# One core, banded attention and a 4-bit feed-forward: dequantization's steps placed behind the first row tiles, b2 copied ahead, transposes fixed behind products, mask loads later

## The chip, the cores and the metric

The kernel runs on one core of one Trainium2 chip. The metric is device time in microseconds (us) of one execution, the median of three runs; the profile is of one further execution, and says when each instruction of each engine began and ended. TensorE (PE) multiplies and transposes, VectorE (DVE) and ScalarE (ACT) work on elements, GpSimd (POOL) does the same for small pieces, SyncE (SP) issues most of the DMAs. Each engine takes its instructions strictly in the order in which they were put into its queue, and waits for semaphores of the others.

## The reference

Four batches of 512 rows of 1024 numbers (2048 rows in all) go through two layers, each followed by a residual sum and a layer norm:

```python
attn = jnp.einsum('ds,td->st', w1, w2) * sparse_mask        # 1024 x 1024, zero outside a band
y    = jax.nn.gelu(jnp.einsum('bds,st->bdt', x, attn) + b2, approximate=False)
x    = _layernorm(x + y)

e    = jnp.linalg.norm(x, axis=-1)
mask = e > 64.0                                             # rows that would take 8-bit weights
y    = where(mask, x @ dequant(qweight, lut8, 8).T, x @ dequant(qweight, lut4, 4).T) + bias
x    = _layernorm(x + y)
```

`dequant` reads bit p of each weight's code from plane p (32 weights to a word) and looks the code up in a table of its own for every output row: 16 entries with 4 bits.

## The kernel before

Rows are handled in 16 tiles of 128 (`x_tiles[0..15]`), columns in 8 blocks of 128 (`KT = 8`) or two halves of 512. The kernel computes the 4-bit product for all rows, and a band of `attn` only; alongside, it checks that no row's norm is over 64 and that the mask is zero outside the band (`outside_band`, `check_outside`, `count_odd`). Were one of the two to fail, `general_path` would compute everything anew. It doesn't with these inputs.

**Stage 1, attn (lines 400 to 486).** Eight column windows s = 0..7, each at most 268 wide: 8 matmuls over k into a PSUM tile (L454), a multiplication by the mask on DVE (L476) into `attn[:, s]`. The matmuls need `w2` transposed: eight tiles of it are loaded by SP into three buffers, transposed on PE into PSUM (L281), and copied to `w2T` by ACT (L282). `w1` comes in pieces of one, one, two, two and two windows into two buffers. The transposes of tile s + 2 stand in the middle of window s, behind its fourth matmul. Beside that the first two row tiles are transposed (`first_xT`).

**Dequantization (lines 281 to 345).** A generator, `dequantize_all`, yields 16 times: twice for each of the 8 blocks of output columns (`ot`). For a pair of blocks DVE first shifts the code words into bytes (`v`, L297, 8 instructions); then for each block and side, ACT computes three entries (`e`, L322) and POOL one (`root`, L326), each as one linear function of bit 0, and DVE selects among them by bits 1 to 3 (L329, L330, L331, L335) and adds the identity to the block of the diagonal (L338), so that the residual comes out of the product. One step later the finished block is transposed on PE and copied by ACT into `wT` (`transpose_pending`). `steps(1)` advances the generator by one yield, and the place of the call in the program decides how soon the scheduler takes its instructions. Before, `steps(1)` stands at the end of each of the 8 windows of stage 1, and 8 more behind the entries of `unpack_after` in stage 2.

**Stage 2, a list of entries `todo`.** Attention of tile n (`attention`): ACT copies b2, spread over all partitions, into a PSUM tile (L526), 10 matmuls add the banded product (L532), ACT applies Gelu (L557), DVE adds the row tile and sums (L561), ACT squares and sums (L380), POOL takes the inverse root (L382, L383), DVE normalizes (L387). "left" and "right" entries are the feed-forward halves of tiles 0 to 3: 8 matmuls of 512 columns (L575), each against one half of `wT`; "left" 0 needs blocks 0 to 3 of `wT`. Each entry's transposed input is prepared one entry ahead (`prepare`). The PSUM tiles of stages 1 and 2 share two buffers (`ps_mm`), the transposes four (`ps_tr`). Row tiles 2 to 11 are loaded into memory that stage 1's tiles leave, so their first load waits for the last of stage 1's instructions.

**Stage 3, pairs of row tiles.** Tiles 4 to 15 go in six pairs through a seven-product form of the 2 x 2 block product (`ffn_pair`, L692). Their inputs are rearranged by `squares`: a DVE transpose in 32 x 32 squares (L642), one DMA out to DRAM (L646) and four back (`rows`, L652), then copies and sums (L674 to L679). `load_outside` loads the parts of the mask outside the band into the places of tiles 0 to 3 (L516), ACT sums their absolute values (L521).

The order within each engine's queue is made by a scheduler from the program's order and its own estimates; from `("attention", 8)` on DVE's is the program's. `tc.issue_after(i)` puts every instruction of its block that goes to the engine of `i` behind `i` in that engine's queue.

Of the kernel before, what the change touches and what calls it, by code (L numbers as in the profile page):

```python
# [9 lines left out]
FP = mybir.dt.float32  # L10
# [7 lines left out]
P = 128  # L18
D = 1024
SOON = 12  # L20
PAIR = 2
KT = D // P
# [11 lines left out]
AHEAD = 2  # L34
# [158 lines left out]
def kernel(  # L193
# [13 lines left out]
    nc = tc.nc  # L207
# [7 lines left out]
    with ExitStack() as main:  # L215
# [48 lines left out]
        b2_bc = const.tile([P, D], FP, name="b2_bc")  # L264
# [20 lines left out]
        def transpose_columns(dst, src):  # L285
            return transpose_blocks(dst, lambda k: src[:, ts(k, P)])
# [81 lines left out]
        def steps(n):  # L368
            for _ in range(n):
                next(low, None)  # L370
# [31 lines left out]
        with tc.tile_pool(name="prod", bufs=1) as prod:  # L402
            w2T = prod.tile([P, KT, D], FP, name="w2T")
            w1_cols = w1.rearrange("(k p) s -> p k s", p=P)
            w2_raw, w1_sb, masks = {}, {}, {}
            first_xT = []

            def load_w2(t):
                w2_raw[t] = prod.tile([P, D], FP, tag="w2", name="w2_raw", bufs=3)
                nc.sync.dma_start(out=w2_raw[t], in_=w2[ts(t, P), :])  # L410

            def load_w1(first, n):

                t = prod.tile([P, KT, n * P], FP, tag=f"w1_{n}", name="w1_sb", bufs=2)
                nc.sync.dma_start(out=t, in_=w1_cols[:, :, first * P : (first + n) * P])
                for s in range(first, first + n):
                    w1_sb[s] = t[:, :, ts(s - first, P)]
                    lo, hi = window(s)
                    masks[s] = prod.tile([P, WIN], FP, tag="mask", name="mask", bufs=6)
                    nc.sync.dma_start(out=masks[s][:, : hi - lo], in_=sparse_mask[ts(s, P), lo:hi])  # L420

            load_w2(0)
            load_w2(1)
            load_w1(0, 1)

            nc.scalar.activation(warm, warm, AF.Gelu)
            load_w2(2)
            load_w1(1, 1)
            load_entries(2, KT, nc.sync)
            load_w2(3)  # L430
            load_w1(2, 2)
            load_codes(0)
            load_codes(1)
            load_w2(4)
            load_codes(2)
            load_codes(3)
            load_w2(5)
            load_w1(4, 2)
            load_w2(6)
            load_w2(7)  # L440
            load_w1(6, 2)
            for n in range(AHEAD):
                load_x(xp0, n)
            nc.sync.dma_start(out=b2_bc, in_=b2.partition_broadcast(P))

            transpose_columns(w2T[:, :, ts(0, P)], w2_raw[0])
            done = transpose_columns(w2T[:, :, ts(1, P)], w2_raw[1])
            behind = ExitStack()
            behind.enter_context(tc.issue_after(done.ins))
            for s in range(KT):  # L450
                lo, hi = window(s)
                ps = ps_mm.tile([P, D], FP, tag="mm", name="mm")
                for k in range(KT):
                    part = nc.tensor.matmul(  # L454
                        out=ps[:, : hi - lo],
                        lhsT=w1_sb[s][:, k, :],
                        rhs=w2T[:, k, lo:hi],
                        start=(k == 0),
                        stop=(k == KT - 1),
                    )  # L460
                    if k == KT // 2 - 1 and s + 2 < KT:
                        with tc.issue_after(part.ins):
                            transpose_columns(w2T[:, :, ts(s + 2, P)], w2_raw[s + 2])
                if s >= KT - 2:


                    for a, b, begins in ((hi - lo, HALF, False), (HALF, D, True)):
                        nc.tensor.matmul(
                            out=ps[:, a:b],
                            lhsT=zeros[:, :P],  # L470
                            rhs=zeros[:, a:b],
                            start=begins,
                            stop=True,
                            skip_group_check=True,
                        )
                nc.vector.tensor_tensor(  # L476
                    attn[:, s, : hi - lo], ps[:, : hi - lo], masks[s][:, : hi - lo], ALU.mult
                )
                if s >= KT - 2 - AHEAD and len(first_xT) < AHEAD:

                    n = len(first_xT)
                    xT = work.tile([P, D], FP, tag="z", name="xT", bufs=2)
                    first_xT.append(xT.rearrange("p (k r) -> p k r", k=KT))
                    transpose_columns(first_xT[n], x_tiles[n])
                steps(1)
            behind.close()

        late = main.enter_context(tc.tile_pool(name="late", bufs=1))
        for n in range(AHEAD, SOON):
# [24 lines left out]
        def load_outside(s):  # L514
            for raw, row, a, b, _ in outside_band(s):
                nc.sync.dma_start(out=raw, in_=sparse_mask[row : row + P, a:b])  # L516

        def check_outside(s):

            for raw, _, _, _, i in outside_band(s):  # L520
                nc.scalar.activation(raw, raw, AF.Abs, accum_out=outside[:, i : i + 1])  # L521

        def band_rows(xT):

            ps = ps_mm.tile([P, D], FP, tag="mm", name="mm")
            nc.scalar.copy(ps, b2_bc)  # L526
            for s in range(KT):
                lo, hi = window(s)
                for h in range(NH):
                    a, b = max(lo, h * HALF), min(hi, (h + 1) * HALF)  # L530
                    if a < b:
                        nc.tensor.matmul(  # L532
                            out=ps[:, a:b],
                            lhsT=xT[:, s, :],
                            rhs=attn[:, s, a - lo : b - lo],
                            start=False,
                            stop=hi == D or (h == 0 and window(s + 1)[0] >= HALF),
                            skip_group_check=True,
                        )
            return ps  # L540
# [31 lines left out]

        def product(ps, xT, h):
            for k in range(KT):
                nc.tensor.matmul(  # L575
                    out=ps,
                    lhsT=xT[:, k, :],
                    rhs=wT[:, k, ts(h, HALF)],
                    start=(k == 0),
                    stop=(k == KT - 1),  # L580
                )
# [49 lines left out]
        def weight_sum(pool, i):  # L631
# [3 lines left out]
            minus = weights[minus] if isinstance(minus, int) else minus  # L635
            nc.vector.tensor_tensor(weights[i], plus, minus, ALU.subtract)

        def squares(pool, n):


            t = pool.tile([P, Q, KT, SQ], FP, tag="squares", name="squares")
            nc.vector.transpose(  # L642
                out=t, in_=x_tiles[n].rearrange("t (c j k) -> t c k j", c=Q, k=KT)
            )
            there = moved.tile([Q, SQ, Q, KT * SQ], FP, tag="there", name="there", bufs=4)
            nc.sync.dma_start(  # L646
                out=there.rearrange("a j c e -> (a j) (c e)"),
                in_=t.rearrange("p c k r -> p (c k r)"),
            )
            rows = pool.tile([P, Q, KT, SQ], FP, tag="rows", name="rows", bufs=2)  # L650
            for c in range(Q):
                nc.sync.dma_start(  # L652
                    out=rows[ts(c, SQ), :, :, :].rearrange("j a k r -> j a (k r)"),
                    in_=there[:, :, c, :].rearrange("a j e -> j a e"),
                )
            return rows.rearrange("p a k r -> p k a r")
# [153 lines left out]
        todo += [("attention", n) for n in range(4 + EARLY, SOON)]  # L810
        for m in range(EARLY):
            todo += [("right", m), ("attention", SOON + m)]
        unpack_after = [("attention", 1), ("left", 0), ("attention", 4), ("left", 1)]
        unpack_after += [("attention", 5), ("left", 2), ("attention", 6), ("left", 3)]

        kept = {}
        rows, blocks = {}, {}
# [14 lines left out]

        def prepare(what, n):
            if what == "attention":
                return first_xT[n] if n < AHEAD else transposed(n, "xT", 2, False)
            if what == "left":
                kept[n] = transposed(n, f"early{n}", 1, True)
            return kept[n]

        ready = prepare(*todo[0])  # L840
# [34 lines left out]
        for n in range(EARLY, NT, PAIR):  # L875
            m = n - EARLY - PAIR
            if 0 <= m < KT:
                for s in range(m, m + PAIR):
                    load_outside(s)
            if n == NT - PAIR:  # L880
                count_all(count_odd())
            ffn_pair(ps_pair, n, blocks[n], lambda part, m=n + PAIR: prepare_pair(m, part))
# [44 lines left out]
```

## Time and profile before

| | |
|---|---|
| three runs | 358.59, 359.25, 360.48 us; median 359.25 |
| the profiled execution, its own time | 360.45 us |
| its span on the core | 358.7 us |
| mean granted clock of TensorE | 0.973 |
| ACT, idle time ahead of its lookups (L322) | 12.6 us, 11.0 of it until DVE's `v` (L297) |
| ACT: 58 to 86 us, 86 to 148 us | busy 19.44 of 28, 53.93 of 62 |
| PE: 58 to 86 us, 86 to 148 us, 148 to 201 us, 201 to 351 us | busy 22.93 of 28, 60.58 of 62, 53.00 of 53, 146.21 of 150 |

In the slices of the page, each digit is the busy share of one fortieth of the span (9 us). A group names its line, engine, operation, result and operands; "idle before" says how long the engine stood idle just ahead of such instructions and what ended it. The granted clock tells at what share of its full rate TensorE was allowed to run.

### The profile page before, as it was taken

The page shows a single profiled execution, that of the slowest core. Times are in us where ns is not written, and L with a number is a line of the kernel's source. Part 1 is how long each engine was busy: PE and PEld are TensorE (multiplying, and loading weights), DVE is VectorE, ACT ScalarE, POOL GpSimd, SP SyncE. Part 2 cuts the span into 40 slices and gives each one's busy share as a digit, 9 for nine tenths or more (in the row PEclk, how much of TensorE's full clock was granted, in tenths as well). Part 3 has the DMA queues.
Part 4 walks back from the last instruction along what each step waited for, and adds up shares of the span by engine and source line. Part 5 has one row for each costly group of instructions (what it writes and reads, how often), then busy time and mean ns, then how long its engine had stood idle before and what let it go on. Part 6 is the DMA issues. An engine that isn't in the chain of part 4 may idle for free.

```text
span 358.7 us, 3719 instructions
## 1 busy us (share of the span) xinstructions
PE 329.9 (92%) x1228; PEld 205.7 (57%) x1228; DVE 214.5 (60%) x341; ACT 179.4 (50%) x257; POOL 90.9 (25%) x131
## 2 busy tenths in 40 slices
PE   7799867598999999999999998999999999999990
PEld 7688756495765759966656643443444443444450
DVE  0589898546997885436476853653644535634342
ACT  3795893978958988974346311303214114024020
POOL 1630431425013442312312530401304004004010
PEclk9899998879999999999999999999999999999996
DMA  8999207700000000320264425153554450441103
GB/s 250 320 320 384 80 0 288 298 2 0 0 0 2 1 0 3 126 111 26 79 215 165 140 80 175 58 199 100 199 177 137 188 175 8 189 154 58 58 3 125
DMA packets 28475, 43.90 MB, mean 122 GB/s; under 512 B 7584, under 2 KB 20640, under 8 KB 28448
## 3 DMA queue, kind: packets, MB, share of 16 engines
q1 hardware_dynamic: 26832, 42.66, 34.9%
q10 hardware_dynamic: 1616, 0.93, 0.9%
q8 instruction: 11, 0.18, 0.2%
q14 instruction: 16, 0.13, 0.1%
HBM read 28.90 MB, written 14.68 MB: 122 GB/s over the span
## 4 chain that ended last, share of the span: by engine, by line
PE 60%; ACT 12%; DMA 11%; DVE 8%; issue 3%; POOL 2%; SPq 2%; ACTq 0%; POOLq 0%; DVEq 0%
PE u L692 15%; PE mm L532 12%; PE mm L575 12%; PE w L692 8%; ACT e L322 6%; PE pt L281 5%; PE v L692 4%; PE mm L454 4%; DMA rows<-there 3%; ACT junk L380 2%; DMA q<-in_L_ffn_qweight_dram 2%; DMA x<-in_L_attn_x_dram 2%; DMA there<-squares 1%; DMA w_sb<-in_L_attn_w_dram 1%; SPq L652 1%
## 5 line engine op out<-in xcount | busy, mean ns | idle before, releaser
L532 PE MATMUL mm<-attn,xT 128*128 128x198 f32 (+2 forms) x320 | 62.5, 353 | 6.9 <-ACT mm L526 6.9
L380 ACT ACTIVATE junk<-x,nm 128x1024 bf16<-128x1024 f32 x31 | 35.7, 1151 | 59.7 <-DVE nm L377 57.3
L532 PEld LDWEIGHTS mm<-attn,xT 128*128 128x128 f32 x320 | 54.8, 197 | 14.6 <-ACT mm L526 7.6
L322 ACT ACTIVATE e<-v,lt,diff 128x1024 f32<-128x1024 uint8 x48 | 56.8, 1243 | 12.6 <-DVE v L297 11.0
L575 PE MATMUL mm<-wT,xT 128*128 128x512 f32 x128 | 56.4, 593 | 1.0 <-ACT wT L282 1.0
L326 POOL TENSOR_SCALAR root<-v,diff,lt 128x1024 f32<-128x1024 uint8 x16 | 31.3, 1965 | 57.9 <-DVE v L297 26.2
L692 PE MATMUL u<-t,halves 128*128 128x512 f32 x96 | 43.3, 593 | 1.0 <-DVE x L712 1.0
L575 PEld LDWEIGHTS mm<-wT,xT 128*128 128x128 f32 x128 | 23.7, 190 | 28.1 <-issue 26.1
L382 POOL TENSOR_SCALAR r<-ss 128x1 f32<-128x1 f32 x31 | 10.4, 334 | 108.8 <-ACT junk L380 108.6
L674 ACT COPY halves<-rows 128x1024 f32<-128x1024 f32 x6 | 6.3, 1048 | 55.4 <-DMA rows<-there 55.4
L454 PE MATMUL mm<-w2T,w_sb 128*128 128x268 f32 (+1 forms) x128 | 30.8, 391 | 2.2 <-ACT w2T L282 2.2
L692 PEld LDWEIGHTS u<-t,halves 128*128 128x128 f32 x96 | 18.2, 190 | 24.3 <-issue 22.5
L678 POOL TENSOR_TENSOR halves<-halves 128x512 f32<-128x512 f32 x6 | 9.5, 1585 | 84.5 <-DVE halves L675 68.3
L642 DVE STREAM_TRANSPOSE squares<-x 128x1024 f32<-128x1024 f32 x12 | 24.3, 2029 | 11.0 <-DMA there<-squares 11.0
L387 DVE TENSOR_SCALAR x<-x,nm,r 128x1024 f32<-128x1024 f32 x16 | 13.0, 813 | 29.0 <-POOL r L383 29.0
L330 DVE COPY_PREDICATED root<-v,e 128x1024 f32<-128x1024 uint8 x16 | 23.3, 1457 | 8.0 <-POOL root L326 4.6
L454 PEld LDWEIGHTS mm<-w2T,w_sb 128*128 128x128 f32 x128 | 23.8, 197 | 6.2 <-ACT w2T L282 2.7
L281 PE MATMUL pt<-ident,x 128*128 128x128 f32 x160 | 21.8, 281 | 4.0 <-DVE x L387 4.0
L561 DVE SCALAR_TENSOR_TENSOR x<-z,x 128x1024 f32<-128x1024 f32 x16 | 21.4, 1335 | 6.2 <-ACT z L557 6.2
L329 DVE COPY_PREDICATED e<-v,e 128x1024 f32<-128x1024 uint8 x16 | 21.3, 1329 | 3.5 <-ACT e L322 3.5
L281 PEld LDWEIGHTS pt<-ident,x 128*128 128x128 f32 x160 | 19.4, 152 | 5.9 <-DVE x L387 4.3
L282 ACT COPY xT<-pt 128x512 f32<-128x512 f32 x40 | 21.4, 591 | 2.3 <-PE pt L281 2.3
(93 smaller groups left out, 438.5 us busy)
## 6 DMA issues: line engine op xcount, KB each, us to landing
x<-in_L_attn_x_dram SPq DMA_DIRECT2D x16, 512.0 KB, 7.4
out_dram<-o SPq DMA_DIRECT2D x14, 512.0 KB, 2.6
there<-squares SPq DMA_DIRECT2D x12, 512.0 KB, 3.1
rows<-there SPq DMA_DIRECT2D x48, 128.0 KB, 2.9
w_raw<-in_L_attn_w_dram SPq DMA_DIRECT2D x8, 512.0 KB, 6.8
w_sb<-in_L_attn_w_dram SPq DMA_DIRECT2D x3, 1024.0 KB, 6.9
w_sb<-in_L_attn_w_dram SPq DMA_DIRECT2D x2, 512.0 KB, 7.2
x<-_L_attn_sparse_mask_dram SPq DMA_DIRECT2D x2, 413.0 KB, 3.7
```

What stands on the lines that cost most here:

```text
L281: nc.tensor.transpose(pt[:, j, :], block(g * (HALF // P) + j), ident)
L282: done = nc.scalar.copy(dst[:, g * (HALF // P) : (g + 1) * (HALF // P), :], pt)
L322: nc.scalar.activation(entry[j], plane(0), AF.Identity, scale=d_k, bias=l_k)
L326: nc.gpsimd.tensor_scalar(entry[j], plane(0), d_k, l_k, ALU.mult, ALU.add)
L330: nc.vector.copy_predicated(root, plane(1), entry[1])
L380: nc.scalar.activation(junk, u, AF.Square, bias=nm, accum_out=ss)
L454: part = nc.tensor.matmul(out=ps[:, : hi - lo], lhsT=w1_sb[s][:, k, :], rhs=w2T[:, k, lo:hi], start=(k == 0), stop=(k == KT - 1),)
L532: nc.tensor.matmul(out=ps[:, a:b], lhsT=xT[:, s, :], rhs=attn[:, s, a - lo : b - lo], start=False, stop=hi == D or (h == 0 and window(s + ...
L561: nc.vector.scalar_tensor_tensor(xt, z, 1.0, xt, ALU.mult, ALU.add, accum_out=total)
L575: nc.tensor.matmul(out=ps, lhsT=xT[:, k, :], rhs=wT[:, k, ts(h, HALF)], start=(k == 0), stop=(k == KT - 1),)
L642: nc.vector.transpose(out=t, in_=x_tiles[n].rearrange("t (c j k) -> t c k j", c=Q, k=KT))
L692: nc.tensor.matmul(out=ps, lhsT=a[:, k, :], rhs=b[:, k, :], start=start and k == 0, stop=stop and k == KH - 1, skip_group_check=True,)
```

## The change

Five edits. (a) The block that keeps ACT's work of dequantization behind the transposes of stage 1 now begins behind the third transposed tile of `w2`, not the second. (b) The last two windows of stage 1 have no `steps(1)`; the steps stand behind attention of tiles 0 to 6 and "left" 0 to 2 instead, ten in all with six in stage 1. (c) The b2 copies of the first two attention entries are written right behind stage 1 (`fill_b2`), ahead of the dequantization steps that follow; further entries copy b2 as before. (d) The transposes that prepare an entry stand behind the last matmul that was traced (`behind_mm`). (e) The mask's loads stand behind the latest `rows` load in SP's queue (`behind_rows`).

```diff
             transpose_columns(w2T[:, :, ts(0, P)], w2_raw[0])
-            done = transpose_columns(w2T[:, :, ts(1, P)], w2_raw[1])
+            transpose_columns(w2T[:, :, ts(1, P)], w2_raw[1])
             behind = ExitStack()
-            behind.enter_context(tc.issue_after(done.ins))
             for s in range(KT):
...
                     if k == KT // 2 - 1 and s + 2 < KT:
                         with tc.issue_after(part.ins):
-                            transpose_columns(w2T[:, :, ts(s + 2, P)], w2_raw[s + 2])
+                            done = transpose_columns(w2T[:, :, ts(s + 2, P)], w2_raw[s + 2])
+                        if s == 0:
+                            behind.enter_context(tc.issue_after(done.ins))
...
-                steps(1)
+                if s < KT - 2:
+                    steps(1)
             behind.close()
+        with_b2 = []
+
+        def fill_b2():
+            ps = ps_mm.tile([P, D], FP, tag="mm", name="mm")
+            nc.scalar.copy(ps, b2_bc)
+            with_b2.append(ps)
+
+        for _ in range(2):
+            fill_b2()
...
+        behind_mm = [part]
+
         def band_rows(xT):
-            ps = ps_mm.tile([P, D], FP, tag="mm", name="mm")
-            nc.scalar.copy(ps, b2_bc)
+            if not with_b2:
+                fill_b2()
+            ps = with_b2.pop(0)
...
-                        nc.tensor.matmul(
+                        behind_mm[0] = nc.tensor.matmul(
                             out=ps[:, a:b],
...
         def product(ps, xT, h):
             for k in range(KT):
-                nc.tensor.matmul(
+                behind_mm[0] = nc.tensor.matmul(
...
+        behind_rows = [None]
         def squares(pool, n):
...
             for c in range(Q):
-                nc.sync.dma_start(
+                behind_rows[0] = nc.sync.dma_start(
...
-        unpack_after = [("attention", 1), ("left", 0), ("attention", 4), ("left", 1)]
-        unpack_after += [("attention", 5), ("left", 2), ("attention", 6), ("left", 3)]
+        unpack_after = [("attention", n) for n in range(7)] + [("left", n) for n in range(3)]
...
             if what == "attention":
-                return first_xT[n] if n < AHEAD else transposed(n, "xT", 2, False)
+                if n < AHEAD:
+                    return first_xT[n]
+
+                with tc.issue_after(behind_mm[0].ins):
+                    return transposed(n, "xT", 2, False)
             if what == "left":
-                kept[n] = transposed(n, f"early{n}", 1, True)
+                with tc.issue_after(behind_mm[0].ins):
+                    kept[n] = transposed(n, f"early{n}", 1, True)
             return kept[n]
...
             if 0 <= m < KT:
-                for s in range(m, m + PAIR):
-                    load_outside(s)
+                with tc.issue_after(behind_rows[0].ins):
+                    for s in range(m, m + PAIR):
+                        load_outside(s)
```

In the queues as they come out, stage 1's first lookups stand behind six copies of `w2T` on ACT, where four stood; the first b2 copy stands right behind the copies of `wT` block 0, the second two lookups later, where 6 lookups and the copies of block 1 stood between. On DVE the mask multiplication of the last window stands three selects and one addition earlier. On PE the transposes of block 1 stand behind the second attention entry, and those of block 4 inside "left" 0. From attention of tile 7 on, PE's order is the same in both. On SP the mask's loads, which stood among the first `out` and `rows` DMAs, stand behind the `rows` of tiles 7, 9, 11 and 13.

## The prediction

> **What bounds the kernel now.** I read the page first. PE is busy 92% of the span, and the slices show that it leaves little after the first fifth; so a change can win what PE stands idle, what it runs at half clock, or nothing.
>
> ```profile
> span 358.7 us, 3719 instructions
> PE 329.9 (92%) x1228; PEld 205.7 (57%) x1228; DVE 214.5 (60%) x341; ACT 179.4 (50%) x257; POOL 90.9 (25%) x131
> ...
> PE   7799867598999999999999998999999999999990
> ...
> PEclk9899998879999999999999999999999999999996
> ```
>
> Next, whom PE waits for. The columns are the waiter, the one waited for, the total, how often, and the longest.
>
> ```profile
> PE mm L532 <- ACT mm L526: 6.9, 3, 5.5
> PE pt L281 <- DVE x L387: 4.0, 1, 4.0
> PE mm L454 <- ACT w2T L282: 2.2, 2, 2.0
> PE u L692 <- DVE x L712: 1.0, 1, 1.0
> PE u L692 <- ACT a L677: 0.9, 1, 0.9
> ```
>
> Two waits hold half of PE's idle time between its first instruction and 350 us (18.2 us, summed over the timeline's brackets): 5.49 us for a b2 copy before attention's first band, 4.04 us for a normalized row tile. The timelines place them and show why the copy is late: ACT works off six lookups and two copies (47.41 to 55.16) that stand ahead of it.
>
> ```profile
> 49.71 1.04 PE L281 MATMUL pt<-ident,root 128*128 128x128 f32 x8
> 56.24 5.33 PE L532 MATMUL mm<-attn,xT 128*128 128x198 f32 x20 [5.49 <-ACT mm L526]
> ```
>
> ```profile
> 47.41 6.92 ACT L322 ACTIVATE e<-v,lt,diff 128x1024 f32<-128x1024 uint8 x6
> 54.21 1.06 ACT L282 COPY wT<-pt 128x512 f32<-128x512 f32 x2
> 55.16 1.98 ACT L526 COPY mm<-b_bc 128x1024 f32<-128x1024 f32 x2
> ```
>
> Idle time costs twice. Below are windows of 3.4 us: length, PE's busy time and instructions, granted clock, DMA share, GB/s. Where PE was busy 1.38 or less of 3.40 us, the next window ran at 0.50; after 1.65 it kept 1.00.
>
> ```profile
> 11.50:14.90 3.40, 1.38 (x9) 0.99 1.15 314
> 14.90:18.30 3.40, 3.40 (x8) 0.50 1.23 330
> 49.10:52.50 3.40, 1.65 (x13) 1.00 0.00 0
> 52.50:55.90 3.40, 0.00 (x0) 0.99 0.11 11
> 55.90:59.30 3.40, 3.06 (x8) 0.51 0.88 337
> ```
>
> **The change, part by part.** I follow the changed queues from stage to stage with durations of this trace. Back to back, the timelines give per instruction: lookup 1.15 us (three in 3.51), copy out of PSUM 0.47, b2 copy and Gelu 0.92, squaring 1.15 to 1.25, select on DVE 1.21, residual 1.22, normalization 0.75; on PE eight transposes 0.87, a band 3.60, a half product 6.87.
>
> *Edit (a).* The copies of the third w2 tile end near 11.9 instead of 15.1, so the 2.02 us wait at 14.72 goes and those matmuls run 12.70 to 14.50. But the next transposes need w2 tile 3, issued at 10.50 and landed 6.7 us later: PE stands from 14.5 to 17.2, where before the transposes began at 18.3. That is 1.1 us ahead if the clock stays, 0.6 behind if it falls (3.4 us at half rate cost 1.7). Either way little reaches the end: DVE's next `v` was done at 37.66, and with the same selects behind the same loads I get 37.7 (38.8 if the clock fell). I take 0, bounds 0 and a 1.1 us loss. The Trainium skill ("TensorE: Matmul & The Clock Gate", Part 1) lets the clock fall only after at least one idle window of some 3.4 us; by it a stop of 2.7 us costs nothing. The trace disagrees: the 2.02 us stop at 12.70 was enough, so I keep the loss as a bound.
>
> *Edits (b) and (c), the first copy.* From 37.75, ACT now runs three lookups (41.2), three copies (42.6), three lookups (46.05), two `wT` copies (47.0) and the b2 copy (47.95). PE, whose last transposes wait for a copy until 41.65, ends stage 1 at 42.1 + 2.7 (three quarters of a window of 3.60) + 2.7 (the last window) + two zero fills of 0.33 = 48.2. The first band starts there, at full clock, and ends at 51.8; before, 56.24 to 61.41. Ahead by 9.6 us.
>
> *What follows the wait.* The row tiles' loads wait for DVE's last mask product (54.39, loads from 54.85). Three selects and an addition fewer put it at about 50.3; the load, 3.3 us from issue to landing, is there at 53.9, and its transposes, which now stand inside the second band, wait 0.6 us. The second band, the transposes of block 1 and of tile 3 end at 58.8, against 66.8. Then comes the new wait. The third b2 copy stands behind, on ACT: Gelu 0 (53.25), lookup, two copies, lookup (56.55), squaring 0 (57.8), Gelu 1 (58.7), lookup (59.85), three copies (61.3), squaring 1, which needs DVE's mean of tile 1 (61.95, behind a normalization, a residual and a select), copy (63.6). It ends at 64.5. So PE stands 5.7 us and restarts at half clock; third band 64.5 against 74.43 before, with 0.87 us of transposes not yet done that were done before.
>
> *Where that goes.* Here ACT and DVE set the pace, not PE: block 3 is finished on DVE at 65.5 (60.9 before), because its steps now interleave with attention. ACT reaches the `wT` copies of blocks 2 and 3 at 79.5; "left" 0 starts there, not at 85.49, after 3.8 us of PE idle. Six of its eight matmuls run, then the transposes of block 4 wait for DVE (about 86.1), and at half clock PE arrives at 86.3 anyway. The fifth band starts at 90.65; before, 93.35. The rest is PE's own work with one wait of 0.7 us for a b2 copy; before it had 0.66 and 0.76 (119.48 and 133.59). Block 5 now is done earlier as well, so both orders have done the same by attention of tile 8: 133.5 against 138.16. **4.66 us ahead**, or 5.96 with no fall of the clock at 79.5.
>
> *Contention.* POOL's lookup takes 1.19 us alone and 2.27 (9.07 for four) where DVE is busy; one took 4.73, and a select took 2.23. Between 60 and 86 us they stand close together (two of block 5 around an inverse root). From nothing to 2 us of the gain; I take 0.46. By the Trainium skill ("SBUF — State Buffer", SBUF: two separate sides) the pair of ports is locked for a whole instruction and the other engine blocks fully. A stretch from 1.19 to 2.27 is about one select's wait, which fits; by it two more such meetings on the path would take 2.4 us.
>
> *Edit (d)* fixes places that the above already contains; nothing more. *Edit (e)*: the mask's loads leave 169 to 205 us, where PE was idle at no time, so their leaving gives 0. Where they go, behind the last `rows`, the SP queue was empty (rows until 221.5, next DMA at 229.96), which hides their issue; without that cover three issues of 0.43 us would delay the next output by 1.3. The waits of stage 3 (0.34, 1.0, 0.88, 0.88) hang on DVE and on PE's order, which stays. I take 0, bounds a gain of 0.4 and the loss of the last rival.
>
> **Sum.** 4.66 - 0.46 = 4.2 us. Against the profiled execution's own 360.45 us (span 358.7 and 1.75 around it) that is 356.25. That execution lies 1.2 above the median of the runs shown; from the median, 359.25 - 4.2 = **355.0 us**.
>
> **Rivals.** *The clock holds, and attention's chain is shorter than I have it.* With 5.96 us, no contention, and 0.4 from the mask's move: 352.9. For it: windows lie anywhere, and 1.65 us busy of 3.4 was enough. Against: 3.8 us of idle time leave few places for the windows that don't see it.
>
> *Half the gain is eaten by ACT and DVE.* ACT was busy 53.93 of 62 us between 86 and 148, and now starts this stretch with more of the dequantization behind it only if block 4 is on time. If the early loss of 1.1 us and 2 us of contention both reach "left" 0, 4.66 - 3.1 leaves 1.6: 357.7. For it: selects on the path, one after another. Against: PE has slack of some 2 us before 79.5.
>
> *Slower: the mask's loads stretch the last `rows`.* Each pair's PE work ends on these rows (249.05 waited for `a` of `rows`, 0.88 us). The loads put right behind them bring 413 + 29 + 349 KB, which at the 410 GB/s of 57 us takes 1.9 us. If rows and mask share the engines evenly, four pairs lose up to 1.9 us each, 7.6 in all: 359.25 - 4.2 + 7.6 = 362.7. It decides from 1.5 us per pair on. For it: that wait has no slack. Against: the rows' descriptors are in the same queue first, and of the five changes of pair only this one waited on them.
>
> **How the numbers follow.** The forecast has 0.5, the held clock 0.2, half the gain 0.2, the mask's loads 0.06, and 0.04 is left for what I don't see. This kernel's runs spread by half a per cent, so I call no change what is within 0.5% (1.8 us: 357.45 to 361.05). The first two are faster, half the gain lies at that edge (0.08 faster, 0.12 the same), the mask's loads are slower; the remainder goes 0.01, 0.03 to same and slower: faster 0.78, same 0.13, slower 0.09. The forecast's own range is 353.8 to 356.4. For 8 in 10 it reaches to the held clock with a little over (351.8) and past half the gain with the loss of 1.1 us (358.8).
>
> **What would show it.** Right: the first band starts between 47 and 50 us at clock 1.00; a new PE wait of 4 to 7 us for ACT's b2 copy before the third band (before 66 us); "left" 0 starting between 78 and 82 us; the normalized tile's 4.04 us wait gone; attention of tile 8 some 4 to 5 us earlier than 138.16, and the same distance at 201.52 and at the end. Wrong: stage 3's waits in sum over 4 us (the mask), or "left" 0 later than 84 us (the dequantization).

## The result and the profile after

The changed kernel takes 361.0 us in the median of 13 runs (359.91 to 363.25), the kernel before 359.14 in 13 runs on the same chip (357.33 to 360.77). The ratio is 1.0051, with a 95% interval from 1.0029 to 1.0073: slower by half a per cent, where 1.2% faster was forecast. The profiled execution took 360.94 us (span 359.2) and lies on its kernel's median; the profiled one of before (360.45) lies 1.3 above its own. So the two profiles differ by 0.5 us of span, the medians by 1.86. Beside the experiments below the kernel before was timed again, with medians of 358.92 to 359.21 us; one of these runs, of 889.45 us, is left out everywhere.

First the page of the kernel after: busy time and two rows of the slices.

```profile
span 359.2 us, 3716 instructions
PE 329.7 (92%) x1228; PEld 204.3 (57%) x1228; DVE 217.2 (60%) x341; ACT 179.2 (50%) x257; POOL 87.6 (24%) x131
...
PE   6699996588999899999999998999999999999990
PEclk9989999696999999999999999999999999999997
```

The sums are nearly those of before. PE's thin places have only moved: the digits 6, 5, 8, 8 from 54 to 90 us, where before 6, 7, 5 stood from 45 to 72. Ahead of the last slice the clock's lowest digits are 6 now, at 63 and at 81 us; before, one 7. Whom PE waits for (waiter, the one waited for, total, how often, longest):

```profile
PE mm L549 <- ACT mm L496: 7.7, 2, 6.3
PE mm L592 <- ACT wT L282: 3.3, 1, 3.3
PE pt L281 <- DMA w_raw<-in_L_attn_w_dram: 2.8, 1, 2.8
```

The waits for ACT (5.5) and for a normalized tile (4.0) of before have become 6.3 us for the third b2 copy, 3.3 us for `wT` and 2.8 us for a load of w2. PE's timeline of after (start, length, then in brackets the idle time before and what ended it) says where:

```profile
49.84 5.40 PE L549 MATMUL mm<-attn,xT 128*128 128x198 f32 x28
...
66.71 6.12 PE L549 MATMUL mm<-attn,xT 128*128 128x198 f32 x20 [6.27 <-ACT mm L496]
...
77.15 1.91 PE L281 MATMUL pt<-ident,root 128*128 128x128 f32 x16
82.33 8.43 PE L592 MATMUL mm<-wT,xT 128*128 128x512 f32 x12 [3.27 <-ACT wT L282]
90.59 1.04 PE L281 MATMUL pt<-ident,root 128*128 128x128 f32 x8
...
94.94 3.76 PE L549 MATMUL mm<-attn,xT 128*128 128x198 f32 x20
```

Against the prediction and the kernel before, starts in us:

| | before | predicted | after |
|---|---|---|---|
| first band | 56.24 | 48.2 | 49.84 |
| third band | 74.43 | 64.5 | 66.71 |
| "left" 0 | 85.49 | 79.5 | 82.33 |
| block 4's transposes (in the middle of "left" 0 only now) | none here | 86.3 | 90.59 |
| fifth band | 93.35 | 90.65 | 94.94 |
| attention of tile 8 | 138.16 | 133.5 | 138.63 |
| stage 3 | 201.52 | 4 to 5 earlier | 201.99 |

A lead of 6.4 us at the first band is 7.7 at the third, 3.2 at "left" 0, and a loss of 1.6 at the fifth. What ACT does in between stands in its timeline of after:

```profile
65.64 1.96 ACT L496 COPY mm<-b_bc 128x1024 f32<-128x1024 f32 x2
70.02 3.50 ACT L322 ACTIVATE e<-v,lt,diff 128x1024 f32<-128x1024 uint8 x3 [2.42 <-DVE v L297]
...
75.28 2.38 ACT L322 ACTIVATE e<-v,lt,diff 128x1024 f32<-128x1024 uint8 x2
...
79.59 1.24 ACT L322 ACTIVATE e<-v,lt,diff 128x1024 f32<-128x1024 uint8 x1
80.72 1.56 ACT L282 COPY wT<-pt 128x512 f32<-128x512 f32 x3
```

The six lookups from 70.02 on are block 4's. That block belongs to the right half, whose first product stands at 157.51. "Left" 0 needs blocks 0 to 3, which DVE had finished at 68.4. Blocks 2 and 3 were transposed on PE at 77.15, behind the late third and the fourth band, and their copies stand in ACT's queue behind block 4's last lookup. On DVE the same shows: the bytes of the third pair came at 68.29 instead of 61.14, and block 4 was done only at 90.11.

```profile
68.29 1.70 DVE L297 TENSOR_SCALAR v<-q 128x256 int32<-128x256 int32 x8
...
89.81 0.38 DVE L338 TENSOR_TENSOR root<-root,ident 128x128 f32<-128x128 f32 x1
```

### The profile page after: what moved, and what is told of

Its sections match the earlier page's. It is cut to its first block, busy times and chain, and to the rows that moved or that the text cites. A ratio compares the mean times of both kernels' runs of the same rounds, so it can differ in the third digit from the quotient of the medians.

```text
span 359.2 us, 3716 instructions
## 1 busy us (share of the span) xinstructions
PE 329.7 (92%) x1228; PEld 204.3 (57%) x1228; DVE 217.2 (60%) x341; ACT 179.2 (50%) x257; POOL 87.6 (24%) x131
## 4 chain that ended last, share of the span: by engine, by line
PE 56%; DMA 12%; ACT 12%; DVE 10%; issue 3%; SPq 2%; POOL 2%; POOLq 0%; ACTq 0%; DVEq 0%
PE u L711 15%; PE mm L592 12%; PE mm L549 9%; PE w L711 8%; ACT e L322 6%; PE pt L281 4%; PE v L711 4%; PE mm L453 3%; ACT junk L380 3%; DMA rows<-there 3%; DMA x<-in_L_attn_x_dram 2%; DMA w_sb<-in_L_attn_w_dram 2%; DMA w_raw<-in_L_attn_w_dram 2%; DMA b_bc<-in_L_attn_b_dram 2%; DMA there<-squares 2%
## 5 line engine op out<-in xcount | busy, mean ns | idle before, releaser
L592 PE MATMUL mm<-wT,xT 128*128 128x512 f32 x128 | 59.5, 619 | 3.3 <-ACT wT L282 3.3
L592 PEld LDWEIGHTS mm<-wT,xT 128*128 128x128 f32 x128 | 24.7, 199 | 31.7 <-issue 28.2
L382 POOL TENSOR_SCALAR r<-ss 128x1 f32<-128x1 f32 x31 | 11.5, 371 | 121.9 <-ACT junk L380 121.8
L326 POOL TENSOR_SCALAR root<-v,diff,lt 128x1024 f32<-128x1024 uint8 x16 | 26.9, 1689 | 47.8 <-DVE v L297 22.8
L453 PE MATMUL mm<-w2T,w_sb 128*128 128x268 f32 (+1 forms) x128 | 29.4, 379 | 1.0 <-DMA w_sb<-in_L_attn_w_dram 1.0
L330 DVE COPY_PREDICATED root<-v,e 128x1024 f32<-128x1024 uint8 x16 | 23.0, 1436 | 4.4 <-POOL root L326 2.8
L578 DVE SCALAR_TENSOR_TENSOR x<-z,x 128x1024 f32<-128x1024 f32 x16 | 20.5, 1283 | 7.0 <-ACT z L574 7.0
L331 DVE COPY_PREDICATED root<-v,e 128x1024 f32<-128x1024 uint8 x16 | 23.7, 1480 | 0.3
L711 PE MATMUL v<-wT,halves 128*128 128x512 f32 x48 | 22.5, 594 | 0.0
```

Of the source, the lines that this page charges most:

```text
L326: nc.gpsimd.tensor_scalar(entry[j], plane(0), d_k, l_k, ALU.mult, ALU.add)
L330: nc.vector.copy_predicated(root, plane(1), entry[1])
L331: nc.vector.copy_predicated(root, plane(2), entry[2])
L453: part = nc.tensor.matmul(out=ps[:, : hi - lo], lhsT=w1_sb[s][:, k, :], rhs=w2T[:, k, lo:hi], start=(k == 0), stop=(k == KT - 1),)
L592: behind_mm[0] = nc.tensor.matmul(out=ps, lhsT=xT[:, k, :], rhs=wT[:, k, ts(h, HALF)], start=(k == 0), stop=(k == KT - 1),)
L711: nc.tensor.matmul(out=ps, lhsT=a[:, k, :], rhs=b[:, k, :], start=start and k == 0, stop=stop and k == KH - 1, skip_group_check=True,)
```

## The experiments

All are edits of the changed kernel. The scheduler makes the queues anew for each of them, so an edit can move other instructions too. Their ratios are to the kernel before, with 95% intervals; the changed kernel's own is 1.0051 [1.0029, 1.0073].

### Is it the early lookups? Edit (a) taken back

```diff
-                            done = transpose_columns(w2T[:, :, ts(s + 2, P)], w2_raw[s + 2])
-                        if s == 0:
-                            behind.enter_context(tc.issue_after(done.ins))
+                            transpose_columns(w2T[:, :, ts(s + 2, P)], w2_raw[s + 2])
...
-            transpose_columns(w2T[:, :, ts(1, P)], w2_raw[1])
+            done = transpose_columns(w2T[:, :, ts(1, P)], w2_raw[1])
             behind = ExitStack()
+            behind.enter_context(tc.issue_after(done.ins))
```

> The changed kernel with edit (a) alone taken back: the lookups start behind the second w2 tile's copies again. Theory 'ACT and DVE set the pace' (the early slip of 1.5 us that the changed kernel showed at ACT 39.26 instead of 37.75 is handed on by ACT and DVE to every later meeting with PE): first band near 48.2 instead of 49.84, 'left' 0 near 80.8 instead of 82.33, median 359.5, that is 1.5 us under the changed kernel's 361.0. Rival 'the clock' (what is lost is lost in half-rate windows around PE's waits, wherever they lie): the first band may come early, but PE then waits longer for the third b2 copy and for 'left' 0, and the time stays within 0.7 us of 361.0.

Measured: 360.6 us, 1.0056 [1.0035, 1.0077]: no difference. The first band came at 48.97, the third already at 62.84, and then PE stood 10.64 us before "left" 0 at 83.56. The theory in its first form, that the early slip is handed on, falls; the rival's figure came, and whether for its reason is asked two runs on. Although the third band moved by 3.9 us, "left" 0 came no earlier; it had four of its sixteen instructions ahead of block 4 (87.59), and the fifth band began at 95.70, 0.8 later than in the changed kernel.

What held "left" 0 here was not ACT's lookups. Its copies (81.97) stood on ACT behind the squaring of tile 3, which waited 3.76 us for DVE's mean; the mean stood behind a normalization that waited 3.01 us for POOL; and POOL's inverse root came at 79.00, behind these lookups of blocks 4 and 5:

```profile
68.95 9.96 POOL L326 TENSOR_SCALAR root<-v,diff,lt 128x1024 f32<-128x1024 uint8 x3
```

Two such lookups took 3.49 us in the changed kernel; why three took 9.96 here stays open.

### Is it the moved steps? Edit (b) taken back

```diff
-                if s < KT - 2:
-                    steps(1)
+                steps(1)
...
-        unpack_after = [("attention", n) for n in range(7)] + [("left", n) for n in range(3)]
+        unpack_after = [("attention", 1), ("left", 0), ("attention", 4), ("left", 1)]
+        unpack_after += [("attention", 5), ("left", 2), ("attention", 6), ("left", 3)]
```

> The changed kernel with edit (b) alone taken back: eight steps of the dequantization in stage 1, the rest behind the same entries as before. Theory 'ACT and DVE set the pace': the first band goes back to about 56, but 'left' 0 finds its weights nearly as in the kernel before and block 4 is there in time; attention of tile 8 at 137.5 to 139 and a median of 359 to 360.5: edit (b) by itself wins nothing and loses 1 to 2 us. Rival 'a moved step is a gain, the third b2 copy's place takes it away': without (b) the time is worse than the changed kernel's, 362 or more, since the early band is lost and nothing regained. Rival 'the clock': as the theory, but with two windows at 0.50 fewer before 100 us.

Measured: 360.59 us, 1.0042 [1.0022, 1.0062]. First band at 57.60, "left" 0 at 88.14 with no wait, fifth band at 95.99, tile 8 at 138.86. Nothing won and nothing lost against the changed kernel: the 7.8 us that (b) brings at the first band are 1.05 at the fifth and 0.2 at tile 8. The first theory's tile 8 came and its median narrowly did not; the rival, which wanted 362 or more, falls. But the kernel without (b) is not the kernel before either; see the run without (a) and (b) below.

### Is it the clock? Products that nobody reads, in PE's gaps

```diff
+        def keep_warm(flat, times):
+            with tc.issue_after(behind_mm[0].ins):
+                for _ in range(times):
+                    behind_mm[0] = nc.tensor.matmul(
+                        out=flat, lhsT=ident, rhs=b2_bc[:, :HALF], start=True, stop=True
+                    )
...
+            if n == 2:
+                pt = ps_tr.tile([P, HALF // P, P], FP, tag="tr", name="pt")
+                keep_warm(pt.rearrange("p a b -> p (a b)"), 6)
             ps = band_rows(xT)
...
+            if n == 0 and h == 0:
+                keep_warm(ps[:, HALF:], 3)
             product(ps[:, :HALF], xT, h)
```

> The changed kernel with products whose result nobody reads in two of PE's gaps: six of 128x512 (about 0.86 us each at full clock) ahead of the third band, three ahead of 'left' 0's product. Theory 'the clock': the windows at 0.50 behind both gaps go; third band 3.6 us long instead of 5.96, 'left' 0's six products 5.16 instead of 8.43; if PE's own time is what decides, tile 8's attention comes 3.3 to 5.7 us before 138.63 and the median is 355.3 to 357.7. Theory 'ACT and DVE set the pace': 'left' 0 begins within 0.5 us of 82.33 and its six products end earlier, but block 4's transposes still wait for DVE (90.11), so PE stands some 2 us there; gain between 0 and 1.5 us, median 359.5 to 361.

Measured: 360.89 us, 1.0064 [1.0040, 1.0087]. The mean granted clock rose from 0.970 to 0.990, and the time did not move. PE's timeline of this kernel:

```profile
67.62 3.76 PE L556 MATMUL mm<-attn,xT 128*128 128x198 f32 x20
...
82.37 5.42 PE L602 MATMUL mm<-wT,xT 128*128 128x512 f32 x12 [2.18 <-ACT wT L282]
90.37 1.06 PE L281 MATMUL pt<-ident,root 128*128 128x128 f32 x8 [2.59 <-DVE root L338]
```

Band and products run at full clock (3.76 and 5.42 instead of 6.12 and 8.43), and PE waits instead: "left" 0 starts as before, and where the slow clock had filled the time until block 4's transposes there is now a wait of 2.59 us for DVE. The extra products made the third band 0.91 us later (67.62), which did not reach "left" 0 either. Here half-rate windows in a gap that others set cost nothing.

### Is it the third b2 copy's place? Copies right behind Gelu

```diff
             nc.scalar.activation(z, ps, AF.Gelu)
+            if n < 2:
+                fill_b2()
             now()
```

> The changed kernel with the third and fourth b2 copies written right behind Gelu 0 and Gelu 1, ahead of what ACT did before them. Theory 'the third b2 copy's place': the wait of 6.27 us before the third band falls to 2 us or less, the third band begins near 60 to 61, and the time falls by 4 to 6 us to 355 to 357. Theory 'ACT and DVE set the pace': the third band begins at 60 to 62, but 'left' 0 waits for its wT copies as long as now (82.3, give or take 1) and block 4 comes at 90, give or take 1; the wait moves from the band to 'left' 0, and the median stays within 1 us of 361.0.

Measured: 365.78 us, 1.0188 [1.0153, 1.0223]: the 6.3 us wait is gone, and the kernel is 4.8 us slower. PE's timeline, and under it ACT's:

```profile
60.22 3.76 PE L549 MATMUL mm<-attn,xT 128*128 128x198 f32 x20
...
82.21 3.78 PE L594 MATMUL mm<-wT,xT 128*128 128x512 f32 x4 [10.01 <-ACT wT L282]
91.57 1.94 PE L281 MATMUL pt<-ident,root 128*128 128x128 f32 x8 [5.58 <-DVE root L338]
```

```profile
72.70 3.50 ACT L322 ACTIVATE e<-v,lt,diff 128x1024 f32<-128x1024 uint8 x3 [0.15 <-DVE v L297]
...
77.24 3.48 ACT L322 ACTIVATE e<-v,lt,diff 128x1024 f32<-128x1024 uint8 x3
80.64 2.00 ACT L282 COPY wT<-pt 128x512 f32<-128x512 f32 x4
```

The third band is 6.5 us earlier and "left" 0 is where it was, to 0.12 us. PE had the transposes ready at 72; the copies that PE needs stand behind six lookups of block 4 (7.0 us of ACT), and in the middle of "left" 0 PE waits again for block 4 itself. Neither theory foresaw the loss. It is worked out at the fifth band, 6.7 us later (101.66): block 4 comes 1.0 later, six products instead of two are still to do behind it (5.94 us against 1.88, 4.1 more), and the sixteen transposes between run at half clock (1.94 and 1.91 us instead of 1.04 each, 1.8 more).

### Block 4's transposes, or block 4's lookups?

With ten steps ahead of "left" 0 block 4 is complete in the program's order, and the line that empties the list of blocks to transpose takes it along. This edit leaves it in the list and keeps the steps. (The right half first reads it at 157.51, not near 200 us as the expectation has it.)

```diff
             if (what, n) == ("left", 0):
-                transpose_pending(0)
+                transpose_pending(1)
```

> The changed kernel, but block 4's transposes (block 4 belongs to the right half, which is first read near 200 us) are no longer put ahead of 'left' 0's last two products; its ten steps ahead of 'left' 0 stay. Theory 'block 4's lookups on ACT, not its transposes on PE' (ACT runs block 4's lookups ahead of the wT copies of blocks 2 and 3, whose selects were done at 68): 'left' 0 still begins at 82.3, give or take 1, its eight products end near 92.6 at half clock, and the median stays within 1 us of 361.0. Rival 'block 4 in the middle of left 0': 'left' 0 ends at 90 or earlier and the median falls by 2 to 3 us to 358 to 359.

Measured: 360.13 us, 1.0037 [1.0005, 1.0070]: 0.9 under the changed kernel, with intervals that overlap. "Left" 0 began at 82.12, ran whole in 8.82 us, 3.4 of it at half clock, and the fifth band came 3.3 us earlier (91.67); but at 120.89 PE waited 2.86 us for DVE, and tile 8 came at 137.65, 1.0 earlier. Taking the transposes out is not shown to be enough.

The other edit puts the steps themselves behind: eight ahead of "left" 0 instead of ten.

```diff
-        unpack_after = [("attention", n) for n in range(7)] + [("left", n) for n in range(3)]
+        unpack_after = [("attention", n) for n in (0, 1, 4, 5, 6, 7)] + [("left", n) for n in range(4)]
```

> The changed kernel with two of the ten steps ahead of 'left' 0 (block 4's) put behind it: stage 1 keeps its six, two stand behind attention 0 and 1, the others behind 'left' 0 to 3 and attention 4 to 7. Five of the six lookups of block 4 still stand ahead of the wT copies on ACT, by the order in which the program is laid out. Theory 'block 4's lookups on ACT': 'left' 0 begins about one lookup, 1.2 us, earlier (81 us), the third b2 copy stays late (third band near 66.7), and the median is 359 to 361. Rival 'too many steps in all ahead of left 0': 'left' 0 begins at 75 to 78 and the median is 356 to 358.

Measured: 357.47 us, 0.9942 [0.9912, 0.9972]: 3.5 us under the changed kernel and faster than the kernel before. PE's timeline:

```profile
66.75 6.40 PE L549 MATMUL mm<-attn,xT 128*128 128x198 f32 x20 [6.09 <-ACT mm L496]
...
81.25 7.13 PE L592 MATMUL mm<-wT,xT 128*128 128x512 f32 x16
...
89.09 3.76 PE L549 MATMUL mm<-attn,xT 128*128 128x198 f32 x20
```

"Left" 0 begins 1.08 us earlier, as the theory had it, yet the gain is the rival's. What the expectation left out: PE's gap there shrank from 3.27 to 0.89 us and the product ran at full clock, eight in 7.13 us (in the changed kernel six in 8.43 and two in 1.88), with no transposes of block 4 between them. The fifth band is 5.85 us earlier. Of these, 3.0 us are left at stage 3's start (199.01).

Last, both together, copies behind Gelu and eight steps:

```diff
             nc.scalar.activation(z, ps, AF.Gelu)
+            if n < 2:
+                fill_b2()
...
+        unpack_after = [("attention", n) for n in (0, 1, 4, 5, 6, 7)] + [("left", n) for n in range(4)]
```

> As the last, and the third and fourth b2 copies right behind Gelu 0 and 1. By the order in which the program is laid out no lookup of block 4 stands any more between Gelu 2 and the wT copies. Theory 'block 4's lookups on ACT' (the third b2 copy was late and the early copy alone lost 5 us, because ACT had six lookups of block 4 ahead of the wT copies): third band near 60, blocks 2 and 3 transposed near 72, 'left' 0 at 74 to 77 instead of 82.2, fifth band at 84 to 88 instead of 94.94, and a median of 354 to 358. Rival 'ACT's and DVE's total is the bound': the work that is put off comes back as waits for b2 copies or residuals between 90 and 138, tile 8's attention stays at 137.5 or later, median 360 to 362.

Measured: 356.69 us, 0.9933 [0.9906, 0.9959]. PE's timeline:

```profile
60.07 3.76 PE L549 MATMUL mm<-attn,xT 128*128 128x198 f32 x20
...
73.88 7.12 PE L594 MATMUL mm<-wT,xT 128*128 128x512 f32 x16
...
81.94 3.86 PE L549 MATMUL mm<-attn,xT 128*128 128x198 f32 x20
...
125.02 5.53 PE L549 MATMUL mm<-attn,xT 128*128 128x198 f32 x20 [4.00 <-ACT mm L496]
```

The early b2 copy that lost 4.8 us is now 8.3 us ahead at "left" 0 (73.88 against 82.21) and 19.7 at the fifth band: block 4's two steps, on ACT six lookups, were the cause. But 7 us of lead over the run before this one shrink to 1.5 us of span (the ratios' intervals overlap), by waits for b2 copies at 125.02 (4.00) and 134.10 (2.68): ACT and DVE have the work that was put off to do there. This part of the rival, ACT's total, was right.

### The steps spread further, and the best version

Same as the last, with the later steps thinner:

```diff
-        unpack_after = [("attention", n) for n in (0, 1, 4, 5, 6, 7)] + [("left", n) for n in range(4)]
+        unpack_after = [("attention", n) for n in (0, 1, 5, 7, 8, 9)] + [("left", n) for n in range(4)]
```

> As the kernel with the steps behind 'left' 0 and the third and fourth b2 copies behind Gelu (356.69), but the eight later steps are spread: behind 'left' 0 to 3 and attention 5, 7, 8 and 9 instead of 4 to 7. In that kernel PE waited 4.0 us at 125 and 2.7 us at 134 for b2 copies that stood on ACT behind three lookups each. Theory 'lookups packed ahead of what PE waits for': both waits fall below 1 us each, the blocks 5 to 7 are still there before the right half's first product (157), and the median falls by 3 to 6 us, to 351 to 354. Rival 'ACT's and DVE's total is the bound': the waits come back later, ahead of the right half's first product, and the median stays between 355.5 and 357.5.

Measured: 355.93 us, 0.9913 [0.9884, 0.9942]: the lowest median of all, with an interval that overlaps those of the two runs before; not the 3 to 6 us that were expected. The two waits went (0.25 at 124.24, 1.32 at 130.30) and others came: 3.48 us for a b2 copy at 139.38, 1.15 for a block on DVE at 145.77. The rival was right. With edit (a) taken back as well, by the first diff above:

> The fastest kernel so far (steps spread, third and fourth b2 copies behind Gelu, 355.93) with edit (a) taken back as well. Theory 'the early start of the lookups costs about 1.5 us where PE waits little behind it': median 354 to 355, with 'left' 0 at 72 to 73 instead of 73.19. Rival 'ACT has no slack to give': the lookups that start earlier with (a) are missing later, PE's waits for b2 copies between 120 and 140 grow by what was won, and the median stays within 0.7 us of 355.9.

Measured: 356.65 us, 0.9918 [0.9892, 0.9944]: no difference, as the rival had it. (The profiled execution, of 358.68 us, was the longest of its seven, and isn't read here.)

### The other edits

Edit (e) alone taken back:

```diff
-                with tc.issue_after(behind_rows[0].ins):
-                    for s in range(m, m + PAIR):
-                        load_outside(s)
+                for s in range(m, m + PAIR):
+                    load_outside(s)
```

> The changed kernel with edit (e) alone taken back: the mask's loads are issued where they were before. Theory: they are hidden in both places; stage 3's four waits stay as they are and the median stays within 0.6 us of 361.0. Rival 'the mask's loads stretch the last rows': without the edit the median falls by 1 us or more.

Measured: 361.1 us, 1.0051 [1.0028, 1.0074]. Hidden in both places; stage 3's waits stay.

Edits (a) and (b) taken back together, by the first two diffs above:

> The changed kernel with edits (a) and (b) taken back; (c), (d) and (e) stay. What is asked: why did the kernel without (b) alone stay 1.5 us above the kernel before? Theory 'the early start of the lookups': (a) makes the first band 1.4 us later (57.60 against 56.24), and here, where PE runs behind it without long waits, this reaches the end: first band at 56.3, give or take 0.4, median 358.5 to 359.6, as the kernel before. Rival 'fixed transposes': the third band keeps a wait of about 5 us for its b2 copy whatever (a) is, and the median stays at 360.2 or more.

Measured: 359.03 us, 0.9995 [0.9972, 1.0018], the kernel before again, with the first band at 55.16 and "left" 0 at 85.86. So (c), (d) and (e) together neither win nor cost. The third band's wait of 4.78 us for its b2 copy is there, so the fixed transposes are not what cost. Edit (a) costs 1.6 us where (b) is absent (360.59 against 359.03, ratios 1.0042 and 0.9995), and nothing where it is present.

Edit (d) alone taken back:

```diff
-                with tc.issue_after(behind_mm[0].ins):
-                    return transposed(n, "xT", 2, False)
+                return transposed(n, "xT", 2, False)
...
-                with tc.issue_after(behind_mm[0].ins):
-                    kept[n] = transposed(n, f"early{n}", 1, True)
+                kept[n] = transposed(n, f"early{n}", 1, True)
```

> The changed kernel with edit (d) alone taken back: the transposes of row tiles find their place freely. By the order in which the program is laid out they then stand further ahead, and block 4's transposes come behind two of 'left' 0's products instead of six. Theory 'block 4's steps set the pace': 'left' 0 at 82 to 84, block 4 at 88 to 92, median within 1 us of 361.0. Rival 'the fixed places cost': median 359.5 or less.

Measured: 362.63 us, 1.0097 [1.0068, 1.0127]. The fixed places are worth about 1.6 us here, with intervals that just overlap, and both expected medians are missed: without them the third and fourth band run together at 66.69, "left" 0 waits 9.11 us until 85.47, and block 4's transposes come behind two products, as in the run with early copies. Edit (c) was not tried by itself.

## Why the prediction was wrong

The miss is 6.0 us. For the profiled execution it is 4.69 (356.25 predicted, 360.94 measured), and it is all there at tile 8: 5.13 us behind the predicted 133.5, of which the sum had set 0.46 aside for contention. The other 1.3 us came with moving the sum to the median.

**The step that failed: "the transposes of block 4 wait for DVE (about 86.1), and at half clock PE arrives at 86.3 anyway", and from it the fifth band at 90.65.** In the sum it is the term of 4.66 us ahead at tile 8, which measured 0.47 behind. Block 4 was ready on DVE at 90.11, 4.0 us late. PE arrived at 90.59, 4.29 late: "left" 0 began 2.83 later, and its six products took 8.26 us, not 6.8, with two windows at half clock where 6.8 leaves room for one. Either holds the fifth band: at full clock, in the run with extra products, block 4's transposes came at 90.37, behind a wait for DVE. From 90.59 to the fifth band it took 4.35 us, exactly what was predicted, so the fifth band's miss of 4.29 lies ahead of these transposes. The mechanism was right (ACT and DVE set the pace there), the size was not. Each link was late, and the delay grew: the bytes of the second pair 1.5 us, the first band 1.6, the third band 2.2, block 3 on DVE 2.9 (68.4 for 65.5), "left" 0 2.8, block 4 4.0. The prediction laid the queue out link by link with durations of instructions back to back, and set 0.46 us aside for all meetings; no run shows that term by itself.

**What the step should have raised.** It saw block 4 in the middle of "left" 0 and only asked when it would be ready, not why PE must wait for a block that nothing reads before 157 us. The runs show that this is the point of the change: with two steps fewer ahead of "left" 0 the same five edits win (0.9942).

**"The rest is PE's own work with one wait of 0.7 us for a b2 copy".** Another 0.84 us came between the fifth band and tile 8, among it a b2 wait of 1.42 instead of 0.7. In the windows between 110 and 130 us of the kernel after (length, then busy time and count of PE, PEld, DVE, ACT and POOL, clock, DMA share, GB/s) ACT and DVE are as good as full:

```profile
110.00:130.00 20.00, 18.58 (x82) 12.19 (x81) 19.25 (x21) 19.40 (x25) 5.54 (x6) 1.00 0.00 0
```

**Edit (a), "I take 0".** The bound was the better value at that place: 1.1 us was named, and the second pair's bytes were 1.5 us late. "The same selects behind the same loads" did not hold: before, DVE did four selects ahead of the second window's mask product (21.20), after it three, and the product came at 21.64. From there to the bytes DVE stood still in neither, so one select more (1.2) and 0.44 us make about the delay. Without (b) the edit costs 1.6 us; in the changed kernel as a whole the run without it shows no cost.

**The median.** The sum was made against an execution at clock 0.973 and carried to a median at which the kernel before runs with fewer half-rate windows. In the 28 runs of it beside the first experiments the four at 0.984 or 0.985 took 357.03 to 357.58 us, and the three at 0.973 or less 359.83 to 360.75. The changed kernel had 0.970 to 0.976 in all 13 runs. So before's profile was a dear one, and it may be that a part of what was counted as gain from its gaps the median did not have to give. This is argued from times and clocks alone; no faster run of the kernel before was traced.

**What held.** First band between 47 and 50 us at full clock; the new wait for the third b2 copy (5.7 predicted, 6.27 measured); the load of w2 tile 3 that stops PE (2.7 and 2.80); the normalized tile's wait gone; edit (e) at nothing. "Left" 0, at 82.33, missed its 78 to 82 narrowly. Of the rivals the nearest was "half the gain is eaten by ACT and DVE": right in kind, and short by 3.3 us (357.7 against 361.0). The sign named for it, "left" 0 later than 84, did not come; the loss lay behind "left" 0's start. The mask's loads were no cause: without edit (e) the kernel takes 361.1.

## What to carry to other kernels

A wait that is removed is won only if the engine that ended it has nothing else that the next consumer needs: follow that engine's queue to the next thing read from it, and ask of each instruction in front of it when its own result is first needed. Work that a late consumer needs should not stand ahead of an earlier one; count the steps that each consumer needs (here eight) and put no more than these ahead of it. If several different removals of waits leave a later start where it was, as "left" 0 at 82 to 84 in five kernels here, look for what that start itself waits for; it need not be the same engine in each (ACT with the copies behind Gelu, POOL without edit (a)).

## What the hardware showed

Half-rate windows follow a grid: in the kernel after the clock falls at about 16.8, 64.5 and 81.6 us, 14 and 5 times 3.41 us apart. Windows of it, 3.41 us long and within 0.1 us of that grid (columns as above; the clock stands third from the right):

```profile
61.24:64.65 3.41, 0.00 (x0) 0.00 (x0) 3.41 (x6) 2.66 (x5) 0.36 (x1) 0.98 1.02 417
64.65:68.06 3.41, 1.35 (x4) 1.24 (x5) 2.68 (x4) 2.95 (x5) 2.46 (x4) 0.50 0.76 306
68.06:71.48 3.42, 3.42 (x13) 3.09 (x12) 2.00 (x11) 1.46 (x2) 1.37 (x3) 0.52 0.00 0
...
78.30:81.71 3.41, 0.76 (x7) 0.52 (x5) 1.45 (x3) 3.41 (x7) 3.23 (x3) 0.98 0.00 0
81.71:85.13 3.42, 2.80 (x4) 1.25 (x5) 2.52 (x4) 2.15 (x5) 1.82 (x5) 0.50 0.00 0
85.13:88.54 3.41, 3.41 (x6) 1.36 (x5) 2.72 (x3) 3.41 (x4) 2.19 (x4) 0.52 0.00 0
```

A window with PE busy 1.35 us or less put the next one at 0.50 to 0.52; with the extra products the emptiest window between 58 and 92 us had 1.58 of 3.41, and the clock stayed at 1.00 in all ten. One idle gap can cost two windows: behind 81.71, PE was busy for 2.80 us and still got 0.52 in the next. The Trainium skill ("TensorE: Matmul & The Clock Gate", Part 1) lets the clock fall after an idle window; here windows in which PE was busy for 0.76 and 1.35 of 3.41 us were enough, so the prediction was right to keep the row. Why 2.80 was too little, while 2.89 between 16.86 and 20.28 brought the clock back, no run here tells.

Where DVE's selects meet POOL's lookups, either can take longer. Before, POOL's first four lookups took 9.07 us and the selects beside them 1.30 to 1.39 each; after, starting within 0.1 us of the same time, POOL took 6.75 and three selects 2.16 to 2.17 each. So a select's duration moved by 0.8 us without any change to either instruction. It is not what made the second pair's bytes late: with selects of 1.34, 1.32 and 2.08 us (block 4's transposes left in the list) the bytes began at 37.26, against 37.46.
